# A graph network on one core: the GRU's n gate by seven block products, one set of accumulator banks for four chains, turned rows by way of DRAM

## The chip, the cores and the metric

The kernel runs on one core of a Trainium2 chip. The metric is the device time of one execution in microseconds; the median of three runs stands for a kernel. A core has a matrix engine (TensorE, PE in the profile; its weight loads are PEld), a vector engine (VectorE, DVE), a scalar engine (ScalarE, ACT), GpSimd (POOL) and a queue processor (SyncE, SP), which here issues nearly all DMAs. Each engine works through its own list of instructions in order and waits on semaphores for the others.

## The reference

128 graphs of 64 nodes with 256 features go through four layers. Each layer takes h = relu(layernorm(x)) and adds its result to x. Cut to what matters here:

```python
h = relu(layernorm(x)); x = x + gat_4_heads(h, adj)      # layer 0
h = relu(layernorm(x)); x = x + gat_1_head(h, adj)       # layer 1
h = relu(layernorm(x)); x = x + relational(h, adj)       # layer 2
h = relu(layernorm(x))                                   # layer 3: three gated steps
for i in range(3):
    m = h @ weight[i]
    aggr = einsum("bst,bsd->btd", A, m)
    gi, gh = aggr @ w_ih.T + b_ih, h @ w_hh.T + b_hh     # r, z, n: 256 columns each
    r = sigmoid(i_r + h_r); z = sigmoid(i_z + h_z)
    n = tanh(i_n + r * h_n)
    h = (1 - z) * n + z * h
x = x + h
```

All values are fp32. In layer 2 the inputs have only the relation 1 (adj is 0 or 1), so one product with the loop weights is left; a general path behind a flag covers other inputs and doesn't run.

## The kernel before

The rows (8192 nodes) are cut into 16 groups of 512: G = 4 blocks of P = 128 rows, two graphs each. Layers 0 to 2 run once for each group, the gated steps three times, 48 steps in all. Products of the steps work on the transposed state hT, two chunks of 128 features by 512 columns; aT is the same for the rows summed over the graph. `wc` is weight[i] times w_ih, made at the start, and `whh` the transposed w_hh.

The order of the work is not that of the program's text. The functions record operations into a `Plan` (lines 222 to 482): each gets a duration from `cost` (line 529) and a due time. A list scheduler then goes forward and backward through them PASSES = 50 times with random ranks and keeps the order that its own arithmetic finds shortest; that order is issued (so nearly all instructions carry line 495). Steps of neighbouring groups alternate (line 1454), and the first three layers of later groups are laid between them.

In a step (`step`, line 940; class `Chunk`, line 946) each chunk c of 128 output features computes r and z together: the 2x2 block product of [r | z] weights with the state (halves S0 and S1 of its columns) is made by seven products instead of eight, in the manner of Strassen and Winograd. `mul` (line 981) holds the seven operands; `weight_sums` (line 854) and `state_sums` (line 862) make the sums that it needs. Products that go to one PSUM bank, `ry`, accumulate, and between them ScalarE reads the sum so far (`m1_there`, `m16_there`, `m165_there`, `r_there`). The bank `rz` holds further parts. Both sources, h and a, add up in the same bank. n is made without this: `gate` (line 1006), for each chunk two products of 512 columns from hT into bank `nh` and two from aT into `ni`. `n_there` and `h_there` finish n and the new state in halves of 256 columns.

PSUM has eight banks (class `Banks`, line 1135): ry, rz, nh and ni have one each, and four (`mt`) serve everything else under the names mm, mn, tp and tq.

Layernorm of groups 2 and later is turned without TensorE (`layernorm_T_by_dma`, line 658): VectorE transposes blocks of 32 x 32, then 16 DMAs move the blocks between partitions, in runs of 32 words:

```python
for i in range(P // S):
    for j in range(P // S):
        ...
        nc.sync.dma_start(turned, blocks[:, :, j * S : (j + 1) * S])
```

`pair` (line 620) picks from the turned rows of the attention and relation layers the 128 columns of two graphs, as weights of a product, in runs of 64 words. A step's state goes back to rows through a DRAM tile `turned` with one DMA out and four back (`back_by_dma`, line 904).

Of the kernel before, what the change touches and what calls it, by code (L numbers as in the profile page):

```python
# [16 lines left out]
S = 32  # L17
# [4 lines left out]
G = 4  # L22
# [199 lines left out]
class Plan:  # L222
# [57 lines left out]
    PASSES, SEED, SPREAD = 50, 57, 50.0  # L280
# [248 lines left out]
def cost(engine, method, args, kwargs):  # L529
# [5 lines left out]
    if engine == "sync" or method == "dma_start":  # L535
        return n * args[0].shape[0] * 4 / 150.0
# [15 lines left out]
def kernel(  # L552
# [45 lines left out]
    mhalf = nc.kept(const, [P, G], F32, name="mhalf")  # L598

# [7 lines left out]
    wsum = nc.kept(const, [P, 1 + LAYERS, 3, D], F32, name="wsum")  # L607
# [4 lines left out]
    def by_graph(hT):  # L612

        return hT.rearrange("p k t -> p (k t)").rearrange("p (a k m j) -> p a k m j", a=2, k=K, j=N)
# [5 lines left out]
    def pair(hT, k, s):  # L620

        return by_graph(hT)[:, s % 2, k, s // 2 * 2 : s // 2 * 2 + 2].rearrange("p r j -> p (r j)")

    def layernorm_T(work, psum, src, hT, natural=None, graphs=False):
# [11 lines left out]
        nc.vector.tensor_scalar(var, mv[:, :, 1], EPS, None, op0=ALU.add)  # L636
        nc.gpsimd.tensor_tensor(rstd, var, mhalf[:, :n], ALU.pow)
        hn = work.tile([P, n, D], F32, name="hn")
        nc.vector.scalar_tensor_tensor(var, mv[:, :, 0], -1.0, rstd, op0=ALU.mult, op1=ALU.mult)
        for p in range(n):  # L640
            nc.scalar.activation(
                hn[:, p, :], src[:, p, :], AF.Identity, bias=var[:, p : p + 1], scale=rstd[:, p : p + 1]
            )
        for k in range(K):
            pt = psum.tile([P, T], F32, name="tp")
            for p in range(n):
                nc.tensor.transpose(pt[:, p * P : (p + 1) * P], hn[:, p, k * P : (k + 1) * P], ident)
            to, out = hT[:, k, :], pt[:, : n * P]
            if graphs:
                to = by_graph(hT)[:, :, k]  # L650
                out = out.rearrange("p (m a j) -> p a m j", a=2, j=N)
            nc.scalar.activation(to, out, AF.Relu)
# [5 lines left out]
    def layernorm_T_by_dma(work, src, hT, natural=None, graphs=False):  # L658
# [10 lines left out]
        nc.vector.tensor_scalar(var, mv[:, :, 1], EPS, None, op0=ALU.add)  # L669
        nc.gpsimd.tensor_tensor(rstd, var, mhalf[:, :n], ALU.pow)  # L670
        nc.vector.scalar_tensor_tensor(var, mv[:, :, 0], -1.0, rstd, op0=ALU.mult, op1=ALU.mult)
        hn = work.tile([P, n, D], F32, name="hn") if natural is None else natural
        for p in range(n):
            to, of = hn[:, p], src[:, p, :]
            if natural is not None:
                to, of = spread(hn[:, :, p : p + 1]), of.rearrange("p (k i b) -> p k i b", k=K, b=S)
            nc.scalar.activation(to, of, AF.Relu, bias=var[:, p : p + 1], scale=rstd[:, p : p + 1])
        tb = work.tile([P, K, n, P], F32, name="tb")
        if natural is None:
            nc.vector.transpose(tb.rearrange("p k n q -> p n k q"), hn.rearrange("p n (k q) -> p n k q", k=K))  # L680
        else:
            for k in range(K):
                nc.vector.transpose(
                    tb[:, k].rearrange("p n (i b) -> p n i b", b=S),
                    hn[:, :, :, k * S : (k + 1) * S].rearrange("p i n b -> p n i b"),
                )
        for i in range(P // S):
            for j in range(P // S):
                turned, blocks = hT[j * S : (j + 1) * S], tb[i * S : (i + 1) * S]
                if graphs:  # L690
                    turned = by_graph(turned).rearrange("p a k m (b c) -> p a b (k m) c", b=2)[:, i // 2, i % 2]
                else:
                    turned = turned.rearrange("p k (n i c) -> p (k n) i c", n=n, c=S)[:, :, i]
                blocks = blocks.rearrange("p k n q -> p (k n) q")
                nc.sync.dma_start(turned, blocks[:, :, j * S : (j + 1) * S])
# [66 lines left out]
    def values(work, psum, src, heads, we, by_dma=False, graphs=False, by_scalar=False):  # L762
# [4 lines left out]
        hT = work.tile([P, K, n * P], F32, name="hT")  # L767
        if by_dma:
            layernorm_T_by_dma(work, src, hT, graphs=graphs)
# [6 lines left out]
        for p in range(n):  # L776
            pm = psum.tile([P, 512], F32, name="mm")
            for k in range(K):
                nc.tensor.matmul(
                    pm[:, : D + 2 * heads], pair(hT, k, p) if graphs else hT[:, k, p * P : (p + 1) * P], we[:, k, :],  # L780
# [50 lines left out]
    def along(psum, hnat, abd, aT, cs):  # L831

        banks = [psum.tile([P, len(cs), G, N], F32, name=name) for name in ("tp", "tq")]
        products = []
        for i, c in enumerate(cs):
            for p in range(G):
                for half, ps in enumerate(banks):
                    b = slice(half * N, (half + 1) * N)
                    for f in range(0, P, N):
                        products.append((ps[f : f + N, i, p, :], hnat[b, (c * P + f) // N, p, :], abd[b, p, :]))  # L840
        beside(products, 355.0 + 467.0 * len(cs))
        to = aT[:, cs[0] : cs[-1] + 1, :].rearrange("p c (g a j) -> p a c g j", a=2, j=N)
        for half, ps in enumerate(banks):
            nc.scalar.copy(to[:, half], ps)

    def weight_sums(w, ws):

        r0, r1, z0, z1 = w[:, 0, :D], w[:, 1, :D], w[:, 0, D : 2 * D], w[:, 1, D : 2 * D]
        nc.gpsimd.tensor_tensor(ws[:, 0], z0, z1, ALU.add)
        nc.gpsimd.tensor_tensor(ws[:, 1], ws[:, 0], r0, ALU.subtract)
        nc.gpsimd.tensor_tensor(ws[:, 2], r1, ws[:, 1], ALU.subtract)
        nc.gpsimd.tensor_tensor(z0, r0, z0, ALU.subtract)  # L860

    def state_sums(m, ms, k):

        if k == 0:
            nc.gpsimd.tensor_tensor(ms[:, 0], m[:, 0, S1], m[:, 0, S0], ALU.subtract)
        else:
            nc.gpsimd.tensor_tensor(ms[:, 2], m[:, 1, S1], m[:, 0, S1], ALU.subtract)
            nc.gpsimd.tensor_tensor(ms[:, 1], m[:, 1, S1], ms[:, 0], ALU.subtract)
            nc.gpsimd.tensor_tensor(ms[:, 3], m[:, 1, S0], ms[:, 1], ALU.subtract)

    def before_recurrence(work, psum, src, adjacency, abd, by_dma=False):

        hT = work.tile([P, K, T], F32, name="hT")
        hnat = work.tile([P, D // N, G, N], F32, name="hnat")
        if by_dma:
            layernorm_T_by_dma(work, src, hT, hnat)
# [5 lines left out]
    class Recurrence:  # L882

        def __init__(self, work, psum, start, src, abd, store):
            self.work, self.psum, self.src, self.abd, self.store = work, psum, src, abd, store
            self.hT, self.hnat = start

        def back(self, c, plus=None, p0=0, n=G, in_parts=False):

            pt = self.psum.tile([P, n, P], F32, name="tp")  # L890
            for p in range(n):
                nc.tensor.transpose(pt[:, p, :], self.hT[:, c, (p0 + p) * P : (p0 + p + 1) * P], ident)
# [11 lines left out]
        def back_by_dma(self, dram):  # L904

            tb = self.work.tile([P, P // S, G, K, S], F32, name="tb")
            for c in range(K):
                nc.vector.transpose(
                    tb[:, :, :, c].rearrange("p j n b -> p n j b"),
                    self.hT[:, c, :].rearrange("p (n j a) -> p n j a", n=G, a=S),  # L910
                )
            turned = dram.tile([P, P // S, G * K * S], F32, name="turned")
            nc.sync.dma_start(turned, tb.rearrange("p j n k b -> p j (n k b)"))
            self.hnat = self.work.tile([P, D // N, G, N], F32, name="hnat")
            for j in range(P // S):
                nc.sync.dma_start(
                    self.hnat[j * S : (j + 1) * S].rearrange("p i n b -> p i (n b)"),
                    turned[:, j].rearrange("(i a) x -> a i x", a=S),
                )

        def ahead(self):

            self.aT = self.work.tile([P, K, T], F32, name="aT")
            along(self.psum, self.hnat, self.abd, self.aT, range(K))
            self.sums()

        def sums(self):
            self.hS = self.work.tile([P, 4, T // 2], F32, name="hS")
            self.aS = self.work.tile([P, 4, T // 2], F32, name="aS")
            for k in range(K):  # L930
                state_sums(self.hT, self.hS, k)
                state_sums(self.aT, self.aS, k)
# [7 lines left out]
        def step(self, i, back=True, in_parts=False):  # L940
# [3 lines left out]
            last = i == LAYERS - 1  # L944

            class Chunk:
# [3 lines left out]
                def __init__(self, c, i, hT, hnew):  # L950
                    self.c, self.i, self.hT, self.hnew = c, i, hT, hnew
                    self.banks, self.first = {}, {}
                    self.r, self.t, self.z = (work.tile([P, T], F32, name=name) for name in "rtz")
                    self.d = self.r

                def bank(self, name):

                    if name in self.banks:
                        return self.banks[name], False
                    self.banks[name] = psum.tile([P, T], F32, name=name)  # L960
                    return self.banks[name], True

                def half(self, name):

                    ps, new = self.bank("rz" if name == "rm" else name)
                    part = ps[:, S1 if name == "rm" else S0]
                    if nc.on:
                        part.region = ps.region
                    return part, new

                def begun(self, name, new):

                    if not nc.on:
                        return
                    name = "rz" if name == "rm" else name
                    if new:
                        self.first[name] = nc.ops[-1]
                    else:
                        nc.ops[-1].after.setdefault(self.first[name], False)
# [788 lines left out]
```

## Time and profile before

| | |
|---|---|
| runs | 1361.50, 1363.83, 1368.96 us; median 1363.83 |
| the profiled execution | 1364.1 us; its span on the core 1362.2 us |
| first matrix products of the steps | from about 90 us on |
| TensorE busy, 120 to 300 us | 177.98 of 180 us |
| TensorE busy, 1320 to 1362 us | 30.97 of 42 us |
| largest waits of TensorE's loads | ry for ScalarE's z 26.7 us, for ScalarE's r 7.5 us |
| DMA packets | 331819, of these 278297 under 512 B |
| DMA issues hT<-hn, hT<-tb | 672 and 224, 32 KB each, 2.0 and 1.9 us to landing |

The profile is one execution. A row of a group names the line, engine, operation and tiles (out<-in), the shapes, how many, and after the bar the busy microseconds and the mean nanoseconds of one, then the engine's idle time just before them and what ended it. An fp32 matrix product shows as two instructions (passes), so 192 products are x384. A matrix instruction's shown length includes its way through the array, which overlaps the next one; from start to start is what it occupies. The timeline's columns are start and length in microseconds.

### The profile page before, as it was taken

The numbers are of one execution on the slowest core, as the hardware profiler recorded it, in microseconds if no ns is written. First come the engines' busy times: TensorE is split into PE (matmuls) and PEld (weight loads), VectorE is DVE, ScalarE is ACT, GpSimd is POOL, SyncE is SP. The second block draws the span as 40 slices with busy tenths as digits, with TensorE's granted clock in tenths as the row PEclk, the third lists the DMA queues.
The fourth block names the chain that finished last, engine by engine and source line by source line (L and its number), as shares of the span: only waits on it lengthen the run. The fifth ranks groups of instructions, "written<-read, shape, count | busy, mean of one in ns | idle before, by whom it ended". The sixth has DMA issues, their size and how long they took to land.

```text
span 1362.2 us, 27169 instructions
## 1 busy us (share of the span) xinstructions
PE 1338.7 (98%) x9319; PEld 928.1 (68%) x9319; DVE 1058.5 (78%) x2627; ACT 776.2 (57%) x1921; POOL 647.4 (48%) x759
## 2 busy tenths in 40 slices
PE   9999999999999999999999999999999999999996
PEld 8666767666676767667676666767666676666674
DVE  6669696977969697896968878797896969676553
ACT  4765666465565655556555665555555565555443
POOL 2444453635554373555426354463645446362632
PEclk9999999999999999999999999999999999999999
DMA  8010323434334343434334343343434333321221
GB/s 228 25 21 19 80 62 71 121 77 114 75 98 108 67 110 87 106 82 100 90 76 117 80 108 79 79 125 64 103 89 97 73 77 98 74 76 61 65 63 34
DMA packets 331819, 115.05 MB, mean 84 GB/s; under 512 B 278297, under 2 KB 324121, under 8 KB 331673
## 3 DMA queue, kind: packets, MB, share of 16 engines
q1 hardware_dynamic: 331112, 112.70, 33.6%
q8 instruction: 77, 1.26, 0.4%
q14 instruction: 70, 0.57, 0.1%
q10 hardware_dynamic: 560, 0.52, 0.1%
HBM read 51.65 MB, written 32.12 MB: 61 GB/s over the span
## 4 chain that ended last, share of the span: by engine, by line
PE 83%; DVE 9%; SPq 2%; ACT 2%; issue 2%; DMA 1%; POOL 1%; DVEq 0%; ACTq 0%
PE ry L495 22%; PE mm L495 16%; PE rz L495 16%; PE nh L495 10%; PE ni L495 10%; PE mm L736 3%; PE tp L736 3%; SPq L495 2%; DVE t L495 2%; DVE hn L495 1%; PE ni L1550 1%; PE tp L495 1%; DVE st L495 1%; DVE r L495 1%; DVE hT L495 1%
## 5 line engine op out<-in xcount | busy, mean ns | idle before, releaser
L495 POOL TENSOR_TENSOR r<-hT,t 128x256 f32<-128x256 f32 x192 | 146.1, 772 | 338.8 <-ACT t L495 338.0
L495 PE MATMUL nh<-hT,whh 128*128 128x512 f32 x384 | 194.1, 595 | 0.5 <-ACT t L495 0.5
L495 PE MATMUL ni<-aT,wc 128*128 128x512 f32 x384 | 193.8, 595 | 0.6 <-ACT aT L495 0.6
L495 ACT ACTIVATE z<-z,brz 128x256 f32<-128x256 f32 x192 | 97.1, 506 | 86.3 <-DVE z L495 85.2
L495 POOL TENSOR_TENSOR aS<-aT 128x256 f32<-128x256 f32 x96 | 75.4, 786 | 134.5 <-ACT aT L495 134.5
L495 ACT ACTIVATE t<-t,bi 128x256 f32<-128x256 f32 x192 | 92.3, 503 | 64.9 <-DVE t L495 62.7
L495 ACT COPY z<-ry 128x256 f32<-128x256 f32 x192 | 70.5, 367 | 101.1 <-PE ry L495 99.9
L495 DVE SCALAR_TENSOR_TENSOR t<-r,t 128x256 f32<-128x256 f32 x192 | 100.2, 530 | 30.9 <-ACT r L495 27.0
L495 PE MATMUL mm<-wl,hT 128*128 128x512 f32 x248 | 119.0, 593 | 0.0
L495 PE MATMUL rz<-hS,whh 128*128 128x256 f32 x384 | 116.9, 386 | 1.7 <-DVE z L495 1.4
L495 PE MATMUL ry<-hS,wsum 128*128 128x256 f32 x384 | 115.7, 383 | 1.0 <-ACT r L495 0.7
L495 DVE TENSOR_TENSOR z<-rz,z 128x256 f32<-128x256 f32 x192 | 79.8, 416 | 46.6 <-PE rz L495 36.9
L495 PE MATMUL rz<-aS,wc 128*128 128x256 f32 x384 | 115.4, 382 | 0.0
L495 PE MATMUL ry<-aS,wsum 128*128 128x256 f32 x384 | 114.8, 381 | 0.2 <-POOL aS L495 0.2
L495 ACT ACTIVATE hn<-xg,var,rstd 128x256 f32<-128x256 f32 x200 | 106.8, 591 | 14.2 <-DVE var L495 13.3
L495 DVE SCALAR_TENSOR_TENSOR r<-z,r 128x256 f32<-128x256 f32 x192 | 104.4, 556 | 12.6 <-POOL r L495 7.2
L495 DVE SCALAR_TENSOR_TENSOR hT<-r,t 128x256 f32<-128x256 f32 x192 | 106.0, 571 | 1.7 <-DVE mv L495 0.4
L495 POOL TENSOR_TENSOR hS<-hT 128x256 f32<-128x256 f32 x96 | 79.4, 830 | 56.8 <-DMA hT<-tb 30.0
L495 PEld LDWEIGHTS ry<-hS,wsum 128*128 128x128 f32 x384 | 70.6, 190 | 51.7 <-issue 26.0
L495 POOL TENSOR_TENSOR rstd<-var,mhalf 128x4 f32<-128x4 f32 (+1 forms) x70 | 73.1, 1046 | 65.0 <-DVE var L495 61.1
L495 POOL TENSOR_TENSOR xg<-xg,hn 128x1024 f32<-128x1024 f32 (+1 forms) x32 | 72.8, 2274 | 59.1 <-DVE hn L495 59.1
L495 DVE BATCH_NORM_STATS2 st<-xg 128x6 f32<-128x256 f32 x256 | 94.2, 407 | 8.0 <-POOL xg L495 5.4
(207 smaller groups left out, 3152.6 us busy)
## 6 DMA issues: line engine op xcount, KB each, us to landing
turned<-tb SPq DMA_DIRECT2D x45, 512.0 KB, 2.9
hnat<-turned SPq DMA_DIRECT2D x180, 128.0 KB, 2.7
hT<-hn SPq DMA_DIRECT2D x672, 32.0 KB, 2.0
xg<-in_x_dram SPq DMA_DIRECT2D x15, 512.0 KB, 4.6
out_dram<-xg SPq DMA_DIRECT2D x15, 512.0 KB
t<-row SPq DMA_DIRECT2D x28, 256.0 KB, 3.6
hT<-tb SPq DMA_DIRECT2D x224, 32.0 KB, 1.9
at<-in_adj_dram SPq DMA_DIRECT2D x64, 32.0 KB, 2.9
```

What stands on the lines that cost most here:

```text
L495: return do(*[real(a) for a in args], **{k: real(v) for k, v in kwargs.items()})
L736: nc.nc.tensor.matmul(*[real(x) for x in product], start=True, stop=True)
L1550: nc.spare = lambda: psum.spare and nc.nc.tensor.matmul(pause, warm, warm, start=True, stop=True)
```

## The change

- n of both chunks is one 2x2 block product, made by seven products of 256 columns for each source (h, a) instead of eight products' worth. The class `Sevens` holds the seven for any gate; a step has four chains of them: n from h, r and z of chunk 0, r and z of chunk 1, n from a. `wsum` grows by the sums for n, and hnew itself carries t.
- The chains share two kinds of bank: `sy` (two banks) for the sums, `sz` (three banks) for the other products. `mt` goes from four to three.
- The new state is finished by two operations over a whole chunk (`done`, 512 columns) instead of two for each half.
- Turned layernorm rows go to a DRAM tile `way` and come back: four DMAs out and four back in runs of 512 B for the attention and relation layers, one out and four back in runs of 1 KB for the recurrence. For the first, the turned state has another layout, in which the columns of two graphs have a step of four words; the transposes on VectorE are two instead of one. Groups 0 and 15 (PLAIN) keep the plain layout of the state, with the 16 DMAs in group 15.
- In layernorm, adding eps and negating the mean move from VectorE to ScalarE, and mean times rstd to GpSimd. ELU's first half goes to ScalarE from group 2 on. The largest edge is taken from row maxima.
- The scheduler's passes, seed and DMA rates are others, and `xg` has five buffers instead of six.

```diff
-    PASSES, SEED, SPREAD = 50, 57, 50.0
+    PASSES, SEED, SPREAD = 35, 71, 50.0
...
-    wsum = nc.kept(const, [P, 1 + LAYERS, 3, D], F32, name="wsum")
+    wsum = nc.kept(const, [P, 1 + LAYERS, 3, D + P], F32, name="wsum")
...
+    def by_graph(work, n):
+
+        return work.tile([P, 2 * P, n // 2, K], F32, name="hT")
...
+    def graphs_of(hT, k, s):
+
+        return hT[:, s % 2 * P : (s % 2 + 1) * P, s // 2, k]
...
-        nc.vector.tensor_scalar(var, mv[:, :, 1], EPS, None, op0=ALU.add)
+        nm = work.tile([P, n], F32, name="nm")
+        nc.scalar.activation(var, mv[:, :, 1], AF.Identity, bias=eps)
+        nc.scalar.mul(nm, mv[:, :, 0], -1.0)
         nc.gpsimd.tensor_tensor(rstd, var, mhalf[:, :n], ALU.pow)
-        nc.vector.scalar_tensor_tensor(var, mv[:, :, 0], -1.0, rstd, op0=ALU.mult, op1=ALU.mult)
+        nc.gpsimd.tensor_tensor(nm, nm, rstd, ALU.mult)
...
+        tb = work.tile([P, 2, P // S, S, n // 2, K], F32, name="tb")
+        for k in range(K):
+            nc.vector.transpose(
+                tb[:, :, :, :, :, k].rearrange("p r j c u -> p u r j c"),
+                hn[:, :, k * P : (k + 1) * P].rearrange("p (u r) (j b) -> p u r j b", r=2, b=S),
+            )
+        way = dram.tile([P // S, 8, S, S * n // 2 * K], F32, name="way")
+        for r in range(2):
+            for a in range(2):
+                nc.sync.dma_start(
+                    way[:, (a * 2 + r) * 2 : (a * 2 + r + 1) * 2].rearrange("j q b x -> (q b) j x"),
+                    tb[a * N : (a + 1) * N, r].rearrange("p j c u k -> p j (c u k)"),
+                )
+        for j in range(P // S):
+            nc.sync.dma_start(
+                hT[j * S : (j + 1) * S].rearrange("p (q c) u k -> p q (c u k)", c=S),
+                way[j].rearrange("q b x -> b q x"),
+            )
...
+            def from_h():
+                n = Sevens(0, "n", (0,))
+                ...
+                seen(0, 0, n.mul("y", 1))
+                add(0, 0, n.mul("m", 2))
+                seen(1, 0, n.mul("y", 6))
+                seen(1, 1, n.mul("y", 5))
+                add(1, 1, n.mul("z", 7))
+                seen(0, 1, n.mul("y", 3))
+                add(1, 0, n.mul("z", 4))
...
+            def gates(c):
+                g = Sevens(c, "r", (0, 1))
+                ...
+                nc.scalar.copy(r[0], g.mul("y", 1))
+                nc.vector.tensor_tensor(r[0], g.mul("m", 2), r[0], ALU.add)
+                r_there(0, r[0])
+                nc.scalar.copy(z[0], g.mul("y", 6))
+                nc.scalar.copy(z[1], g.mul("y", 5))
+                z_there(1, g.mul("z", 7))
+                r_there(1, g.mul("y", 3))
+                z_there(0, g.mul("z", 4))
+                return r, z, rs, zs
+
+            def done(d, z, to):
+                nc.vector.scalar_tensor_tensor(d, z, 1.0, d, op0=ALU.add, op1=ALU.mult)
+                nc.vector.scalar_tensor_tensor(to, d, 0.5, to, op0=ALU.mult, op1=ALU.add)
...
+            from_h()
+            from_a([gates(c) for c in range(K)])
...
-            own = ("ry", "rz", "nh", "ni")
+            own = ("sy", "sz")
...
-                return {"mt": 4, "ry": 1, "rz": 1}.get(tag, 1)
+                return {"mt": 3, "sy": 2, "sz": 3}.get(tag, 1)
...
-            xg = work.tile([P, G, D], F32, name="xg", bufs=6)
+            xg = work.tile([P, G, D], F32, name="xg", bufs=5)
...
-            elu_add(pool, src, o, nc.vector if g < 1 else nc.gpsimd, g < 0)
+            elu_add(pool, src, o, nc.vector if g < 1 else nc.gpsimd, g >= AHEAD)
...
+        PLAIN = (0, NG - 1)
```

## The prediction

> **What bounds the kernel now.** I read the page from the top: shares of busy time, then the chain of work that ended last, then the groups by shape, and last the timeline, for what one product costs when the queue runs.
>
> ```profile
> span 1362.2 us, 27169 instructions
> ...
> PE 1338.7 (98%) x9319; PEld 928.1 (68%) x9319; DVE 1058.5 (78%) x2627; ACT 776.2 (57%) x1921; POOL 647.4 (48%) x759
> ...
> PE 83%; DVE 9%; SPq 2%; ACT 2%; issue 2%; DMA 1%; POOL 1%; DVEq 0%; ACTq 0%
> ```
>
> TensorE is busy 98% of the span and is 83% of the chain that ended last, and the slices show it at full clock. Busy time overstates a pipelined engine, so I take prices from start to start (here TensorE alone):
>
> ```profile
> 650.35 1.02 PE L495 MATMUL ni<-aT,wc 128*128 128x512 f32 x2
> 651.20 0.59 PE L495 MATMUL ry<-hS,wsum 128*128 128x256 f32 x2
> 651.63 0.59 PE L495 MATMUL ry<-aS,wsum 128*128 128x256 f32 x2
> 652.07 0.59 PE L495 MATMUL rz<-hT,whh 128*128 128x256 f32 x2
> ```
>
> A product is two passes (x2). One of 512 columns holds TensorE 0.86 us (650.35 to 651.20), one of 256 columns 0.43 us (651.20 to 651.63): no price for being narrow. The groups of n and of the engines that follow:
>
> ```profile
> L495 PE MATMUL nh<-hT,whh 128*128 128x512 f32 x384 | 194.1, 595 | 0.5 <-ACT t L495 0.5
> L495 PE MATMUL ni<-aT,wc 128*128 128x512 f32 x384 | 193.8, 595 | 0.6 <-ACT aT L495 0.6
> L495 PEld LDWEIGHTS mm<-w0e,hT 128*128 128x128 f32 x248 | 46.6, 190 | 11.4 <-issue 3.3 <-PE ry L495 0.5 <-PE rz L495 0.4
> L495 DVE TENSOR_TENSOR t<-t,ni 128x256 f32<-128x256 f32 x192 | 74.7, 413 | 15.4 <-PE ni L495 14.4
> L495 DVE SCALAR_TENSOR_TENSOR hT<-r,t 128x256 f32<-128x256 f32 x192 | 106.0, 571 | 1.7 <-DVE mv L495 0.4
> L495 DVE STREAM_TRANSPOSE hn<-hn 128x1024 f32<-128x1024 f32 x42 | 52.0, 1238 | 6.0 <-ACT hn L495 5.5
> ```
>
> And what a turn in an accumulating bank costs where nothing else lies in the queue (the last step, all engines):
>
> ```profile
> 1340.61 0.59 PE L495 MATMUL ry<-aS,wsum 128*128 128x256 f32 x2
> ...
> 1341.30 0.35 ACT L495 COPY z<-ry 128x256 f32<-128x256 f32 x1
> ...
> 1341.71 0.70 PE L495 MATMUL ry<-hT,wsum 128*128 128x256 f32 x2 [0.51 <-ACT z L495]
> ```
>
> The next product into the bank must wait until ScalarE has read the sum so far. It could have started at 1341.04 (1340.61 + 0.43) and started at 1341.71: 0.67 us lost. So each such turn wants 0.67 us of other products in between.
>
> Priced so, TensorE's queue before comes to some 1310 us (products as above; from the same timeline 0.445 and 0.435 us for 264 and 258 columns, 0.11 us for a transpose of 128, 1.08 us for the 32 small products of an aggregation over the graph, 0.54 to 1.05 us for those of an attention or the relation, 0.135 us per warming pass). The other 50 us or so of the 1362.2 are gaps, unfilled turns among them.
>
> **What the Trainium skill says.** "TensorE: Matmul & The Clock Gate", section "Wait — 56ns, not 53.3ns?", gives N/1.2 GHz, or N/2.4 GHz plus 2.5 ns, from start to start. The trace has 0.215 us per pass of 256 at full clock, which is N/1.2 plus 2 ns for each of the two fp32 passes; the measurement decides. "PSUM — Partial Sum Buffer", Terms ("PSUM bank"): two engines must not be in one bank and quadrant at once. That is the turn above. "SBUF — State Buffer", section "SBUF: two separate sides": lines of 16 bytes, at least two hits on a line for full bandwidth; no row here shows a weight load with a step of 16 bytes. "DMA: Bandwidth & Descriptors", Specifications: full rate from 512 B on. The page has 278297 of 331819 packets under 512 B, yet the DMA engines are only about a third busy.
>
> **The change part by part.** There are 48 steps (16 groups, 3 layers).
>
> *n by seven products.* Removed per step: 4 nh and 4 ni products of 512 columns, 8 x 0.86 = 6.88 us. Added: 7 + 7 of 256 columns, 14 x 0.43 = 6.02 us. 48 x 0.86 = **-41.3 us of TensorE**, the engine that bounds. r and z keep 28 products. Weight loads rise by 288 x 2 passes x 0.19 us, and stay hidden where the 256-wide rows hide theirs today (190 ns under 215).
>
> *Turns.* n now has turns as well, two chains per step, but PSUM is dealt out anew: two banks sy and three sz in place of one each of ry, rz, nh, ni; mt goes from four to three. In the instruction order of the changed kernel I counted turns with less than 0.67 us of other TensorE work between: 90 before (58 us short in sum), 70 after (41 us short). Before, 58 us short went with about 50 us of gaps, not all of them turns, so 17 us less short is worth between 0 and -14 us; I take -6.
>
> *Three banks for the rest.* The rows of mm, tp and mn show 0.0 to 0.6 us of idle in all, so four were ample. A pair of banks is wanted some 128 times (eight per group: four for the two attentions, one for the relation, three for the aggregations), each held for about 1.2 us of reading (two of 0.16 and 0.41). At 0 to 0.2 us each: 0 to +26 us; I take +3.
>
> *VectorE.* Out per step: 10 additions at 0.42 and 12 fused operations at 0.55, in all 505 us from six rows (100.2 + 104.4 + 106.0 + 79.8 + 40.1 + 74.7). In, over all steps: 768 additions at 0.415 (319 us), 192 fused at 0.53 (102), 192 fused of 512 elements at about 0.80 (154; 0.53 plus 256 elements at the 1.05 ns that lie between the transposes of 512 and 1024, 701 and 1238 ns). Sum 575, +70. Away: both var rows, -51; the minimum of ELU for 28 groups of rows, 28 x 0.776 = -22; the edge maximum, -5; the transposes are cut in two, 84 x 0.70 for 52.0, +7. Net about 0: 1058 us over some 1320 is 80%. It stays cover, with less slack.
>
> *ScalarE* gets the var and nm operations (70 each, about 0.2 us: 27 us) and ELU's first half (28 x 1.05 = 29 us); its step work is 454 us before and after. 832 us, 63%. *GpSimd* gets 70 small products and 16 weight sums, about +30 us, 51%. Both hidden. The layernorm path gets two short ScalarE operations and one on GpSimd in place of two on VectorE; it feeds work due many microseconds later.
>
> *Turned rows through DRAM.* 42 tiles at 16 issues each become 4 + 4; 13 of the 14 at the recurrence's start 1 + 4. The 16 held SP's queue 11.50 us in the timeline (0.72 each); eight cost about 5, plus landings of 2.9 and 2.7: some 10.5 us for 13.5 to the last row. SP's wait between writing and reading back stands ahead of loads and stores with more than that to spare. The two DRAM tiles named way now serve 100 uses instead of 45, at about 10 us each: 40% full. I take 0.
>
> *Step of 16 bytes.* In the new hT of the attention and relation layers a weight column lies 4 words from the next (14 groups with four row blocks). Between the 64- and 128-column loads (133, 190 ns) a column costs 0.89 ns. Lower bound: nothing. Upper: every column at twice that, 190 to 304 ns, which the loads' start with the pass before exposes as about 0.105 us on the 224 + 224 passes of 264 and 258 columns: +47 us; 512-wide passes hide it. I take 0, since the load already moves a column in more than a cycle and may absorb the second line access. The same step on the transposes' writes would cost VectorE up to 84 x 0.54 = 45 us (83%): hidden.
>
> *The end.* The last step has no other group beside it. Its n chains add turns, and the final update works on 512 elements instead of 256: +2 us.
>
> Sum: -41.3 - 6 + 3 + 2 = -42.3 on 1362.2, so a span of 1320 and a time of 1321.8, as the profiled execution took 1364.1; the median of the three runs shown, 1363.83, is the same to 0.3 us. **1322 us.**
>
> **Rivals.** (1) *The banks bind*: three mt banks and shared accumulators, +26 us in place of +3 and no gain from fuller turns: 1322 + 23 + 6 = 1351. For it: the gain needs every other engine on time, and VectorE goes to 80%. Against: today's idle before these rows is nothing. (2) *Strided weights, the slower side*: full price of 47 us plus the 10 us that rising VectorE writes and later reads then cost: 1322 + 57 = 1379. It decides from -42 us up: 42/448 = 0.094 us per pass, that is loads of about 290 ns. For it: the line rule above; against: a load is latency for its first part and no row shows the penalty. (3) *Better than priced*: SP's freed queue and the fuller turns take a further quarter of the 50 us of gaps: 1310. That the change doesn't do what it says I exclude: the queue holds 28 + 14 products of 256 per step and none of nh or ni.
>
> **How the numbers follow.** Forecast 0.62 (1312 to 1338), banks 0.17 (1338 to 1360), strided weights 0.11 (1360 to 1395), better 0.10 (1300 to 1312). The range 1305 to 1358 leaves out the strided case and the edges of two others, about 0.18. Telling from no change takes 0.5%, 7 us: 1357 to 1371. Faster: 0.62 + 0.10 + 0.14 of the banks' 0.17 = 0.86; same: the other 0.03 and 0.02 from the cheap end of the strided case; slower: 0.09.
>
> **What would show it.** TensorE's passes of 256 still 0.215 us from start to start, x672 more products and no 512-wide ones but the relation's: the main term. Weight loads of mm near 190 ns: no stride penalty; near 300, and 0.3 us from start to start on w0e and w1e: rival 2. Idle before mm, mn, tp rows above some 10 us: rival 1. VectorE near 1058 us, transposes near 0.70 us, ScalarE near 830. I am wrong if the TensorE sum falls by 40 us and the span does not.

## The result, and the profile after

The changed kernel takes 1356.83 us (median, 1355.3 to 1357.78) against 1363.6 for the kernel before on the same chip: a ratio of 0.9949, 95% interval 0.9937 to 0.996. It is faster, but by 7 us where 42 were forecast. The head of its page:

```profile
span 1353.9 us, 28083 instructions
...
PE 1322.5 (98%) x9893; PEld 1078.5 (80%) x9893; DVE 1080.9 (80%) x2598; ACT 818.1 (60%) x2089; POOL 686.9 (51%) x845
```

TensorE is as full as before, on a span only 8.3 us shorter. VectorE has 23 us more than the forecast 1058. The timeline of TensorE shows the products that n is now made of:

```profile
650.17 0.59 PE L495 MATMUL sy<-hT,whh 128*128 128x256 f32 x2
650.60 0.59 PE L495 MATMUL sy<-aT,wc 128*128 128x256 f32 x2
651.03 0.59 PE L495 MATMUL sy<-hS,wsum 128*128 128x256 f32 x2
```

One starts every 0.43 us, as priced. So TensorE's time, taken from start to start, was split in three for every kernel: products at their own price, the sets of small 64-row products, and gaps (what a start is later than the price of the product ahead of it). The ends of the span make up the rest. Another choice of the prices, by a ns or two, moves the single sums by about 1 us.

| us | before | after | difference | forecast |
|---|---|---|---|---|
| products at their price | 1197.0 | 1156.6 | -40.4 | -41.3 |
| sets of small products | 106.7 | 112.7 | +6.0 | 0 |
| gaps | 50.4 | 76.0 | +25.6 | -1 |
| before the first and after the last product | 8.1 | 8.8 | +0.7 | |

The products went as forecast. Of their 40.4 us, 25.6 came back as gaps and 6.0 in the sets of small products, where the forecast had nothing of the kind. The groups by shape, of the operations that the prediction priced:

```profile
L495 DVE STREAM_TRANSPOSE hn<-hn 128x512 f32<-128x512 f32 x84 | 88.5, 1119 | 9.3 <-ACT hn L495 9.0
L495 DVE SCALAR_TENSOR_TENSOR r<-z,r 128x512 f32<-128x512 f32 x96 | 88.0, 918 | 14.4 <-POOL r L495 7.0 <-ACT z L495 5.0 <-ACT fs L495 1.2
L495 DVE SCALAR_TENSOR_TENSOR hT<-r,hT 128x512 f32<-128x512 f32 x96 | 79.4, 829 | 1.1
L495 DVE STREAM_TRANSPOSE tb<-hT 128x512 f32<-128x512 f32 x90 | 61.8, 695 | 2.6 <-DMA way<-tb 2.0 <-DMA hT<-tb 0.2
L495 PEld LDWEIGHTS mm<-w0e,hT 128*128 128x128 f32 x248 | 60.5, 309 | 3.4 <-issue 1.1 <-DVE hnat L495 0.3 <-ACT es L495 0.3
```

Two transposes of 512 elements stand side by side: tb<-hT, written without the new step, takes 695 ns; hn<-hn, written with a step of 16 bytes, 1119. The weight loads from the same layout take 309 ns where they took 190. The loads are at the prediction's upper price, the transposes near it. Yet the passes that the loads feed are hardly later. The timeline of the first 16 of a tile of w1e, loads (PEld) and passes (PE), before:

```profile
371.37 3.46 PEld L495 LDWEIGHTS mm<-w1e,hT 128*128 128x128 f32 x16
371.59 3.65 PE L495 MATMUL mm<-w1e,hT 128*128 128x258 f32 x16
```

and after:

```profile
1009.31 3.81 PEld L495 LDWEIGHTS mm<-w1e,hT 128*128 128x128 f32 x16
1009.52 3.90 PE L495 MATMUL mm<-w1e,hT 128*128 128x258 f32 x16
```

Sixteen passes take 3.90 us in place of 3.65, 16 ns each. Sixteen loads of 0.31 us would be 5.0 us one after the other; they take 3.81, so they overlap one another. Over all products, gaps below 40 ns sum to 9.5 us after and 1.4 before. That is what shows of the loads.

What TensorE waited for after, in us, times and longest:

```profile
PE tp L495 <- DVE hT L495: 9.8, 4, 3.6
PE mm L495 <- DMA hT<-way: 4.1, 4, 1.4
PE sz L495 <- DVE hT L495: 2.8, 6, 0.7
PE sy L495 <- DVE hT L495: 2.0, 4, 0.8
```

The first row was 2.7 us before. It lies where transposes on TensorE directly follow a step: two such places are within the span (at 132 and 1322 us, some 3.7 us each) and one at the end. Right after the first of them the granted clock is half for 3.4 us (0.50 from 131.8 to 135.2 us), and a pass of 256 columns takes 427 ns in place of 215; the kernel before has full clock there. This adds 1.6 us to the gaps. The second row is turned rows that come late. The third and fourth are products of the steps that wait for VectorE's work on the state (hT); the kernel before shows 1.3 us of waits for hT there. All waits that this view lists sum to 23.0 us, against 16.0 before: they name 7 us of the 25.6, and the short gaps at the loads another 8. What ended the rest isn't shown.

### The profile page after: what moved, and what is told of

Same layout as the page of the kernel before. It is cut to its first block, busy times and chain, and to the rows that moved or that the text cites. A ratio compares the mean times of both kernels' runs of the same rounds, so it can differ in the third digit from the quotient of the medians.

```text
span 1353.9 us, 28083 instructions
## 1 busy us (share of the span) xinstructions
PE 1322.5 (98%) x9893; PEld 1078.5 (80%) x9893; DVE 1080.9 (80%) x2598; ACT 818.1 (60%) x2089; POOL 686.9 (51%) x845
## 4 chain that ended last, share of the span: by engine, by line
## 5 line engine op out<-in xcount | busy, mean ns | idle before, releaser
L495 POOL TENSOR_TENSOR r<-hT,hT 128x256 f32<-128x256 f32 x192 | 154.6, 812 | 321.0 <-ACT hT L495 320.1
L495 DVE SCALAR_TENSOR_TENSOR hT<-r,hT 128x256 f32<-128x256 f32 (+1 forms) x288 | 177.6, 622 | 30.6 <-ACT r L495 28.0
L495 PE MATMUL sy<-aS,wsum 128*128 128x256 f32 x576 | 173.6, 384 | 1.0 <-DVE hT L495 0.9
L495 PE MATMUL sz<-hS,whh 128*128 128x256 f32 x576 | 171.4, 383 | 1.6 <-DVE hT L495 1.4
L495 PE MATMUL sy<-hS,wsum 128*128 128x256 f32 x576 | 172.0, 384 | 0.0
L495 PE MATMUL sz<-aS,wc 128*128 128x256 f32 x576 | 164.6, 382 | 0.6 <-DVE hT L495 0.4
L495 DVE TENSOR_TENSOR hT<-hT,sz 128x256 f32<-128x256 f32 x288 | 119.1, 414 | 42.0 <-PE sz L495 40.7
L495 PEld LDWEIGHTS sz<-hS,whh 128*128 128x128 f32 x576 | 107.3, 190 | 24.6 <-issue 5.5
L495 PEld LDWEIGHTS sy<-aS,wsum 128*128 128x128 f32 x576 | 106.7, 190 | 24.0 <-DVE hT L495 5.4
L495 PEld LDWEIGHTS sz<-aS,wc 128*128 128x128 f32 x576 | 106.9, 190 | 18.3 <-DVE hT L495 1.3
L495 ACT ACTIVATE hn<-xg,nm,rstd 128x256 f32<-128x256 f32 x200 | 108.2, 593 | 10.2 <-POOL nm L495 8.5
```

Of the source, the lines that this page charges most:

```text
L495: return do(*[real(a) for a in args], **{k: real(v) for k, v in kwargs.items()})
```

## The experiments

A theory and its rival stand in the text on record with each. Times are medians; the kernel before ran beside each batch and took 1363.8 to 1365.2 us. "The step" is the distance of a weight column to the next in the attention and relation layers: 16 bytes in the changed kernel.

### The step, n and the way through DRAM, each undone

**Step of 8 bytes.** The block pair u moves outside the columns in hT, tb and way. The runs through DRAM shrink to 256 B. The order of the instructions on the engines stays.

```diff
-        return work.tile([P, 2 * P, n // 2, K], F32, name="hT")
+        return work.tile([P, n // 2, 2 * P, K], F32, name="hT")
...
-        return hT[:, s % 2 * P : (s % 2 + 1) * P, s // 2, k]
+        return hT[:, s // 2, s % 2 * P : (s % 2 + 1) * P, k]
```

> The changed kernel, but the turned rows of the attention and relation layers have a column step of two words (8 bytes) instead of four (16 bytes), by another order of the same values; DMA runs of 256 B instead of 512 B there. The orders on TensorE, ScalarE and GpSimd stay the same. Theory A (the step of 16 bytes costs): weight loads of mm fall from about 310 to about 190 ns, the 84 transposes from 1119 to about 700 ns (VectorE 35 us less busy), and the time falls by 8 to 20 us, to some 1343. Rival B (the turns in the shared banks and the three banks left for the rest eat the gain): loads and transposes may get shorter, but the time moves by less than 3 us.

**n undone alone.** Two 512-wide products per chunk and source for n, in the changed kernel.

```diff
+            def plain_n(name, w, m, c):
+                ps = psum.tile([P, P // S, P], F32, name=name)
+                f = 2 * D + c * P
+                for k in range(K):
+                    nc.tensor.matmul(ps, w[:, k, f : f + P], chunk(m, k), start=(k == 0), stop=(k == K - 1))
+                return ps
```

> The changed kernel with n alone undone: n from h and from a by two products of 512 columns for each chunk again, in one sy bank and one sz bank; its weight sums are left away. All else as changed, planned anew. If the seven products save what TensorE's start-to-start times say, the time rises by 25 to 41 us, to 1382 to 1398. Rival B (n's turns give the saving back): the time rises by less than 12 us, and the gaps on TensorE get fewer by some 30 us.

**Both.**

> The kernel with the step of 8 bytes and runs of 256 B (1338.8 us), and in it n undone as in the second experiment: two 512-wide products per chunk and source; the weight sums of n are left out. Theory A (the step of 16 bytes and n by seven products are two separate prices): n is again worth some 24 us, so 1361 to 1365. Rival B (the longer VectorE work of the 16-byte step is what kept n from its full 40 us): 1376 to 1381.

**The way through DRAM undone** in the attention and relation layers, with the weight columns side by side.

```diff
-        return work.tile([P, 2 * P, n // 2, K], F32, name="hT")
+        return work.tile([P, 2, K, n * N], F32, name="hT")
...
+        for i in range(P // S):
+            for j in range(P // S):
+                turned = hT[j * S : (j + 1) * S].rearrange("p a k (m b c) -> p a b (k m) c", b=2, c=S)[:, i // 2, i % 2]
+                blocks = tb[i * S : (i + 1) * S].rearrange("p k n q -> p (k n) q")
+                nc.sync.dma_start(turned, blocks[:, :, j * S : (j + 1) * S])
```

> The changed kernel, and in the attention and relation layers alone the turned rows as before: one transpose of 1024 elements per tile, 16 DMAs inside SBUF, weight columns side by side. Everything else stays changed (n by seven, banks, the moved small operations, the recurrence's rows through DRAM). Theory A (the way through DRAM is neutral but for its 16-byte step): 1334 to 1344, weight loads at 190 ns, transposes 1238 ns. Rival B (the way through DRAM itself saves time by freeing SP's queue, and the step hid that): 1345 to 1353. Rival C (the way through DRAM itself costs, rows come late): 1326 to 1333.

| us | n by eight | n by seven | worth of seven |
|---|---|---|---|
| step of 16 bytes | 1381.23 | 1356.83 | -24.4 |
| step of 8 bytes | 1367.73 | 1338.80 | -28.9 |
| rows inside SBUF, columns side by side | | 1347.00 | |

The step of 8 bytes has a ratio of 0.9812 (0.9792 to 0.9832) to the kernel before, and theory A holds: the 16-byte step cost 18 us, or more if the shorter runs cost anything. Its page and groups:

```profile
PE 1308.9 (98%) x9893; PEld 1041.0 (78%) x9893; DVE 1056.4 (79%) x2598; ACT 817.1 (61%) x2089; POOL 686.3 (51%) x845
```

```profile
L495 DVE STREAM_TRANSPOSE hn<-hn 128x512 f32<-128x512 f32 x84 | 55.8, 694 | 11.5 <-ACT hn L495 10.8
L495 PEld LDWEIGHTS mm<-w0e,hT 128*128 128x128 f32 x248 | 47.8, 196 | 10.0 <-issue 2.2 <-DVE u L495 1.0 <-ACT es L495 0.6
```

Transposes and loads are back at their short durations (694 and 196 ns), and VectorE at 1056.4 us. The gaps fall from 76.0 to 61.4 us: the small ones from 9.5 to 2.6, so 7 us of the 18 were loads showing; the large ones from 66.5 to 58.8. The sets of small products fall by 2.7.

n by seven takes 40 us from TensorE's products in either setting and saves 24 or 29. Both runs just missed their ranges. The second is 24.4 us slower, 0.8 short of the range for a saving that arrives, and far from its rival's 12. The third, at 1367.73 us, lies between theory A (1361 to 1365) and rival B (1376 to 1381), and nearer to A: the two prices are nearly separate. Everything in the change but n and the step comes in sum to 3 us or so: with n by eight and the step of 8 bytes the ratio to the kernel before is 1.0025 (1.0015 to 1.0034). Single parts may cancel in it.

Without the way through DRAM the time is 1347.0, between its two forms. So theory A falls, and the time is in rival B's range: the way through DRAM is worth 8 us with a step of 8 bytes (1347.00 to 1338.80) and costs 10 with one of 16 (to 1356.83). This run has an order of its own, so some of the 8 may be the planner's, and that SP's freed queue is the reason isn't shown.

### What is chance

Two runs change only what should not matter, the planner's passes and seed (35 and 71 to 50 and 57) at either step. A third deals the banks out otherwise (mt four, sz two in place of three and three).

```diff
-    PASSES, SEED, SPREAD = 35, 71, 50.0
+    PASSES, SEED, SPREAD = 50, 57, 50.0
```

> The changed kernel with the scheduler's passes and seed of the kernel before (50, 57). Nothing of the work differs, only the order found. It gives the size of the planner's luck: under both theories within 5 us of 1357; if it moves by more than 8 us, single comparisons of planned kernels say little below that.

> The changed kernel with four mt banks and two sz banks instead of three and three. Theory A: no gain, 1353 to 1362, since the chains lose a bank. Rival B in its form that three mt banks are short: 5 to 15 us faster, with less idle before mm, tp and mn.

> The kernel with the step of 8 bytes and the planner's passes and seed of the kernel before (50, 57): how much of the difference between two plans is chance. If chance is small, 1336 to 1341, and the seventh experiment's 1348 is the price of its edit; if it is large, 1343 to 1350, and the seventh can't be told from it.

They took 1354.61, 1356.27 and 1340.91 us. Another order alone is worth some 2 us in these two trials. Four mt banks at the price of one sz bank gain nothing. In that run the sets of small products are 4.8 us shorter than in the changed kernel and the gaps 6 us longer, so the third bank alone, without a bank taken elsewhere, isn't priced.

### VectorE's load

**The transposes done one and a half times.** At the step of 8 bytes, half of each transpose is written once more into the same place, so that VectorE holds the transposes as long as the 16-byte step did, with the loads left short. The order stays.

```diff
             nc.vector.transpose(to, of)
+            if nc.on:
+                def twice(first, to, of):
+                    first()
+                    nc.nc.vector.transpose(real(to), real(of))
+                op = nc.ops[-1]
+                op.call = partial(twice, op.call, to[:, 0], of[:, 0])
```

> The kernel with the step of 8 bytes, and in it after each of the 84 transposes of the attention and relation layers half of it once more into the same place, about 0.43 us of VectorE each (694 to about 1119 ns, the duration that the 16-byte step had); the weight loads stay near 196 ns and the order of the work on all engines stays. Theory A (the 18 us of the 16-byte step came over VectorE's longer transposes): 1352 to 1358. Rival B (they came over the weight loads of 303 to 314 ns): 1338 to 1342. In between, the two share it in that proportion.

**The same after every other transpose.**

> The sixth experiment with the second, half transpose after every other transpose only: 19 us more on VectorE than at the step of 8 bytes, in place of 38 (which cost 33). Theory (a knee: the order hides VectorE up to about what it was laid for, and from there on each us costs one): 1341 to 1350, less than half of 33. Rival (every us of VectorE from 1056 us up costs the same): 1354 to 1357.

**Less on VectorE elsewhere.** The minima with the edges are left out of the attentions (50 fewer operations in the trace, where the expectations say 48), first at the step of 8 bytes, then at 16, the order of the rest unchanged.

```diff
                 nc.vector.tensor_tensor(t4, t4, edges, ALU.min)
+                nc.ops[-1].call = lambda: None
```

> The kernel with the step of 8 bytes (1338.8 us, VectorE 1048 us), and in it one VectorE operation left out of each attention, the minimum with the edges (48 operations of 0.72 and 0.45 us, together about 29 us; what lies beside an edge is then not masked), with the order of all else unchanged. Theory (VectorE bounds stretches of the time, and the 38 us added in the sixth experiment cost 33 for that reason): 1314 to 1325. Rival (VectorE is hidden up to about 1050 us and decides only above it): 1333 to 1340.

> The changed kernel (1356.8 us, VectorE 1081 us), and in it the 48 minima with the edges left out as in the ninth experiment (20 us less on VectorE there, which gained nothing at the step of 8 bytes; what lies beside an edge is not masked), all else in the same order. Theory (the part of the 18 us that isn't exposed weight loads, some 10 us, came since VectorE went over what the order can hide): 1345 to 1351. Rival (it came over something else of the step, and VectorE's busy time doesn't count here either): 1354 to 1358.

| | VectorE busy | time | against the same kernel without the edit |
|---|---|---|---|
| 8 bytes, 84 half transposes more | +33.0 | 1372.05 | +33.3 |
| 8 bytes, 42 half transposes more | +15.6 | 1350.40 | +11.6 |
| 8 bytes, no minima | -19.6 | 1338.68 | -0.1 |
| 16 bytes, no minima | -17.9 | 1356.22 | -0.6 |

(The expectations say 1048 us for VectorE at 8 bytes; its page has 1056.4.) The first row is more than either theory allowed, and the first three together look like a knee of VectorE's load, as expected of the second. The last row decides against that: the changed kernel would be past the knee, and 18 us less on VectorE gain it nothing. What the rows with a cost share is the place: the work sits between the layernorm and the turned rows. (The run with 42 ends 0.4 us above its range, far from its rival's.) The waits of TensorE at 8 bytes without the edit:

```profile
PE tp L495 <- DVE hT L495: 9.8, 4, 3.6
PE mm L495 <- DMA hT<-way: 5.7, 5, 2.0
```

and with the 84 half transposes:

```profile
PE mm L496 <- DMA hT<-way: 11.7, 11, 2.7
PE tp L496 <- DVE hT L496: 9.8, 4, 3.6
PE sz L496 <- DVE hT L496: 5.7, 10, 1.1
PE sy L496 <- DVE hT L496: 4.7, 7, 1.8
```

The rows arrive later (5.7 to 11.7 us), and products of the steps (sz, sy) wait for VectorE's work on the state (0.8 us without the edit, 10.4 with it), some of which stands right behind the transposes in its queue. Together that is some 16 of the 33 us. Two things stay open. Work taken from one place was compared with work added in another; no run adds time to the minima, so the place is argued, not shown. And the 16-byte step makes the transposes as long, in the same order, but costs only 18 us with its loads: why the added half transposes cost 33 wasn't found.

**The right price in the planner.** The changed kernel with its 16-byte step, and in `cost` the transposes at what they take.

```diff
+        if method == "transpose" and any(isinstance(v, View) and v.base.tag == "hn" for v in args[:1]) and n == 512:
+            return 1120.0
```

> The changed kernel with its step of 16 bytes, and in the planner alone the price of its 84 transposes at 1120 ns as measured, in place of 682: the order can now be laid with VectorE's true load. Theory (the step costs much since the order was laid for transposes of 682 ns; the 7 us of exposed loads stay): 1345 to 1350. Rival (VectorE's time is short whatever the order): 1354 to 1359.

1343.41 us, a ratio of 0.985 (0.9833 to 0.9866): better than the theory's range, 13.4 us below the changed kernel. The operations are as slow as ever:

```profile
L495 DVE STREAM_TRANSPOSE hn<-hn 128x512 f32<-128x512 f32 x84 | 89.2, 1115 | 7.5 <-ACT hn L495 7.3
L495 PEld LDWEIGHTS mm<-w0e,hT 128*128 128x128 f32 x248 | 59.5, 310 | 2.3 <-ACT wh L495 0.4 <-ACT nm L495 0.2 <-issue 0.2
```

and the late rows are gone:

```profile
PE tp L495 <- DVE hT L495: 10.0, 4, 3.7
PE sy L495 <- ACT r L495: 1.8, 2, 1.1
...
PE mm L495 <- DMA hT<-way: 0.5, 1, 0.5
```

The late rows aren't what the 18 us hang on, though: at the step of 8 bytes, in the changed kernel's order, there are 5.7 us of them. What both faster kernels lack is waits of the step's products for VectorE's work on the state: 4.8 us in the changed kernel, 0.8 at the step of 8 bytes, none here. The large gaps fall from 66.5 to 54.2 us; the small ones stay at 9.2. So most of the 18 us came because the order was laid for transposes of 682 ns, and what is left of the step against 1338.8 us is about 5, near the 7 of the loads that show. The three other orders at this step (1354.6, 1356.3, 1356.8) make chance an unlikely reason for 13 us.

### Late rows and late new state

Six runs at the step of 8 bytes tried to take the two largest waits of TensorE away. In the planner alone: half the rate for the DMAs of way; a later landing for them; the fused operations of 512 elements at 870 ns.

```diff
-        rate = 300.0 if isinstance(to, View) and to.base.tag == "way" else 150.0
+        rate = 150.0 if isinstance(to, View) and to.base.tag == "way" else 150.0
...
-            rate = 180.0
+            rate = 90.0
```

> The kernel with the step of 8 bytes, and in the planner's cost alone half the rate for the DMAs to and from the DRAM tile (150 and 90 B/ns in place of 300 and 180), so that it lays the turned rows' path earlier. Theory (the rows come late because the plan takes them for faster than they are): TensorE's wait of mm for the DMA of hT falls from 5.7 us to under 2 and the time to 1332 to 1336. Rival (another order of the same quality, and the lateness has another cause): 1337 to 1342, the wait stays above 4 us.

```diff
-                op.end = wire + 400.0
+                op.end = wire + (1200.0 if any(b.tag == "way" for b in op.bases) else 400.0)
```

> The kernel with the step of 8 bytes, and in the planner alone 1200 ns in place of 400 between the wire and the landing for DMAs of the DRAM tile way. In the eighth experiment the halved rate also filled the planner's one wire for all DMAs, which this doesn't. Theory (turned rows come late since the plan takes them for faster than they are): TensorE's wait of mm for the DMA of hT falls from 5.7 us to under 2, and the time to 1332 to 1336. Rival: 1337 to 1345, another order with as much waiting elsewhere.

```diff
+        if method == "scalar_tensor_tensor" and n == 512 and not any(v.base.pool.psum for v in args if isinstance(v, View)):
+            return 870.0
```

> The kernel with the step of 8 bytes, and in the planner alone 870 ns in place of 682 for the fused VectorE operations of 512 elements in SBUF (192 of them, measured 915 and 832 ns). Theory (the plan overloads VectorE because it prices these too low, 36 us in all): 1326 to 1334. Rival (VectorE's lateness is spread over contention that no price describes): 1336 to 1345.

In the kernel: plain n in the three steps before transposes; there the new state in halves; and the halves with both prices together, planned in 50 passes.

```diff
+            (plain_from_h if back else from_h)()
+            (plain_from_a if back else from_a)([gates(c) for c in range(K)])
```

> The kernel with the step of 8 bytes, and n by plain 512-wide products in the three steps alone that transposes on TensorE follow directly (group 0 step 0, group 15 steps 1 and 2); four small copies of weights more at the start. Theory (there the new state comes late since both chunks of n end together): TensorE's wait for hT before transposes falls from 9.8 to 3 to 5 us, TensorE gets 3 x 0.86 = 2.6 us more, so 1333 to 1337. Rival (the wait only shows that the end is late for other reasons, and moves to another row): 1338 to 1342.

```diff
+                def finish(c, hs):
+                    if not back:
+                        done(*gated[c][2:], chunk(hnew, c))
+                        return
+                    for h in hs:
+                        done(gated[c][0][h], gated[c][1][h], t[c][h])
...
-                done(*gated[1][2:], chunk(hnew, 1))
+                finish(1, (1, 0))
```

> The eleventh kernel (step of 8 bytes, fused operations of 512 elements priced at 870 ns in the planner; 1336.9 us), and in the three steps that transposes on TensorE follow directly the new state finished in halves of 256 columns, the early half first, instead of 512. Theory (there the last 512-wide operations lie on the path): TensorE's wait for hT before transposes falls from 10.6 us to 6 to 8, and the time to 1332 to 1335. Rival (what is saved there is lost in another place): 1336 to 1339.

> The fourteenth kernel with the later landings of the tenth in the planner and 50 passes: whether the parts that each took a wait away add up. If waits of TensorE add up to time: 1328 to 1333. If a floor of some 60 us of gaps stays whatever wait is removed: 1334 to 1339.

| at the step of 8 bytes | late rows | tp for hT | all gaps | time |
|---|---|---|---|---|
| no edit | 5.7 | 9.8 | 61.4 | 1338.80 |
| later landing | 0.5 | 11.1 | 59.6 | 1338.37 |
| fused operations at 870 ns | 0.8 | 10.6 | 58.9 | 1336.90 |
| plain n in three steps | 5.0 | 5.8 | 65.6 | 1348.10 |
| halves, with 870 ns | 5.3 | 4.2 | 66.4 | 1345.38 |
| halves, 870 ns, later landing | below 0.5 | 6.1 | 61.9 | 1339.75 |

A planner's price removes the late rows, as the theory of the later landing said, but gains 0 to 2 us, as the rivals did. For instance TensorE's waits with the later landing:

```profile
PE tp L495 <- DVE hT L495: 11.1, 5, 4.2
PE sy L495 <- DVE hT L495: 1.6, 2, 1.4
...
PE mm L495 <- DMA hT<-way: 0.5, 1, 0.5
```

The new state comes earlier with halves (the wait falls to 4.2), and the time rises, beyond both ranges, as it did with plain n:

```profile
PE mm L495 <- DMA hT<-way: 5.3, 7, 1.6
PE tp L495 <- DVE hT L495: 4.2, 4, 2.1
...
PE sy L495 <- ACT var L495: 2.2, 1, 2.2
PE sy L495 <- DVE hT L495: 2.1, 1, 2.1
PE sy L495 <- ACT r L495: 2.1, 1, 2.1
```

Three waits of 2 us in other places took its room. Each edit makes the planner lay another order, and two of these lost 7 to 9 us, more than the seeds did; whether by the edit or by the order isn't settled. Gaps stay between 59 and 66 us whatever single wait goes, as the rival of the last run said; its time, 1339.75, is 0.8 us above that rival's range and far above the theory's.

The halved rate took 1461.57 us. In the planner all DMAs share one wire, and the lower rate may have filled it; that was not tried apart. It shows how far a wrong price in `cost` reaches: +123 us with the same work. The clock has a part in it: the mean granted clock is 0.961 (0.996 in the changed kernel), with stretches at half clock such as 607.5 to 613.0 us, where a pass of 256 columns takes 427 ns. Products then cost some 31 us more than at full clock.

The fastest kernel measured is the one with the step of 8 bytes and 870 ns in the planner: 1336.90 us, ratio 0.9798 (0.9781 to 0.9814).

## Why the prediction was wrong, by its steps

It had the direction and the main product term; what it named as proof against itself, TensorE's sum down by 40 us and the span not, is what happened. The time is 35 us above the forecast. Of these the step of 16 bytes is 18 (1356.83 to 1338.80), the part of n's saving that didn't arrive at the step of 8 bytes 12 (28.9 of 41.3), and what remains, about 5, is the rest of the change, forecast at -1 and measured at +4 (1367.73 against 1363.6).

The largest step that failed is one of its terms: *step of 16 bytes*, "I take 0", with the transposes' longer writes called hidden. The upper prices it worked out for the operations were near: 304 ns for a load (303 to 314 measured) and 0.54 us more for a transpose (0.42). What was wrong is where they would show. The loads, feared at 47 us, show 7, while their records overlap one another. The transposes, called hidden on an engine at 80%, carry most of the other 11: the run with nothing but their right price in the planner brings back 13, so the order, laid for 682 ns, made most of the cost. VectorE's share of busy time didn't tell of this.

The Trainium skill had the rule. "SBUF — State Buffer", section "Specifications (TRN2)", wants two hits on each 16-byte line for full bandwidth. The runs agree: one hit (16 bytes) gives 309 ns, two (8 bytes) 196, four (side by side) 190. The prediction quoted it and set it aside on an argument (a column already takes more than a cycle and may absorb the second access) for which no profile it had showed a strided load.

*n by seven products*, the second step that failed: -41.3 on TensorE, -40.4 measured. That the span would follow was wrong: 24 to 29 us of it arrived. At the step of 8 bytes the gaps grow by 7.6 us (53.8 to 61.4) when n goes from eight to seven: removed products may also be cover that is no longer there; that this is the reason isn't shown. TensorE's waits for hT before transposes are part of it (7.3 to 9.8); the rest is spread.

*Turns*, -6: none in the changed kernel (gaps ahead of products into the accumulating banks: 28.6 us before, 28.7 after), 19.4 at the step of 8 bytes. That is the size forecast, but only there, so it stood under the condition that the step's other work keeps time.

*Three banks*, +3: not settled. The list of waits has no long one of mm, tp or mn for a reader of their banks, but the sets of small products grew by 6.0 us against a forecast of nothing; the step of 8 bytes takes 2.7 of that back, the run with four mt banks 4.8. *ScalarE and GpSimd*, 832 us and +30: 818 and +39. *VectorE*, 1058: 1080.9, of which 29.7 are the transposes (88.5 us busy where 84 at 0.70 make 58.8) and 13 the fused operations of 512 elements (918 and 829 ns in place of 0.80 us); the rest came out lower.

*Turned rows through DRAM*, 0: worth some 8 us without their step, if the order has no part in it. *The end*, +2: none at the very end. Its two last waits are 2.02 and 0.70 us, where they were 2.25 and 0.43:

```profile
1343.77 0.69 DVE L495 SCALAR_TENSOR_TENSOR hT<-r,hT 128x512 f32<-128x512 f32 x1
...
1344.61 0.63 PE L495 MATMUL tp<-ident,hT 128*128 128x128 f32 x4 [2.02 <-DVE hT L495]
...
1345.94 0.63 PE L495 MATMUL tp<-ident,hT 128*128 128x128 f32 x4 [0.70 <-DVE hT L495]
```

But the two other places of this kind, which the prediction overlooked, wait 3.6 and 3.8 us each, where the kernel before shows no such wait; no edit brought this back as time.

Of the rivals, strided weights named the right cause at three times its size: 47 us for the loads, which show 7, and 10 for the longer writes, for which about 11 are left.

## What to carry to other kernels

When an order is laid by prices, a change in layout that slows an operation must be told to the planner: here one price was worth 13 us, with the same operations. A share of busy time does not tell whether an operation is hidden; ask what stands behind it in its queue and who waits for its result (that the place decides was argued here, not shown). And of what is taken from a bounding engine, expect only a part: here 24 to 29 of 40 us arrived, and the rest went into new gaps.

## What was not expected of the hardware

- An fp32 weight load of 128 columns takes 190 ns with columns side by side, 196 with a step of 8 bytes and 303 to 314 with 16, but in a row of loads and 258-column passes the 16-byte step shows only as 16 ns per pass. Passes of 512 columns, said by the prediction to hide it, are longer too: 437 ns from start to start in the mean with 16 bytes, 430 with 8.
- A 32x32-block transpose of 512 elements takes 694 ns when its writes have a step of 8 bytes, 1119 with 16.
- A fused VectorE operation of 512 elements in SBUF takes 0.69 us at the end of the run, where GpSimd has nothing to do, and 0.83 to 0.92 us on average. That GpSimd's work at the same time is the reason was not tried.
- Small operations on [128, 4] cost 296 ns on ScalarE (var) and 279 ns on GpSimd (nm).
